# Whitened 2-D convolution: the last three channel groups image by image, x in three tiles, and 1024 consecutive columns at a time in the last pass

## The chip, the cores and the metric

The kernel runs on one core of one Trainium2 chip. The metric is the device time of one execution in microseconds; the time of a kernel is the median of its runs. A core has five engines that matter here: PE (TensorE, matmuls, with its weight loads shown as PEld), DVE (VectorE), ACT (ScalarE), POOL (GpSimd) and SP (SyncE, which here only issues DMAs). 16 DMA engines carry all transfers, whichever engine issued them.

## The reference

Two layers are computed, on `x` of shape (4, 64, 256, 256): 4 images, 64 channels, 256 x 256 pixels.

Layer 0 is a long convolution per channel. Its kernel is an outer product of two filters of length 256 (`hx` and `hy`, each made by a small network of three sine layers and an exponential decay):

```python
k = jnp.einsum('ijk,imk->ijmk', hx, hy)[0]
k = jnp.transpose(k, (2, 0, 1))
k_f = jnp.fft.rfft2(k, s=(fft_size, fft_size)) / fft_size
u_f = jnp.fft.rfft2(x.astype(jnp.float32), s=(fft_size, fft_size))
y = jnp.fft.irfft2(u_f * k_f, s=(fft_size, fft_size))[..., :L, :L]
out = y + x * bias[:, None, None]
```

Since the kernel is separable, this is a product with a lower triangular Toeplitz matrix along one axis of the image and a second one along the other.

Layer 1 whitens the 64 channels over all images and pixels:

```python
x1 = jnp.transpose(x, (1, 0, 2, 3)).reshape(B, -1)
x1_s = x1[:, ::STRIDE ** 2]
mean1 = jnp.mean(x1_s, axis=-1, keepdims=True)
xc = x1 - mean1
cov = x1_s @ x1_s.T / x1_s.shape[1] + EPS * jnp.eye(B, dtype=x.dtype)
deconv = _isqrt_newton_schulz(cov, N_ITER)
out = deconv @ xc
```

The mean and the covariance are taken from every ninth pixel. The inverse square root of the 64 x 64 covariance comes from five Newton-Schulz iterations. No output can be computed until all images have been through layer 0 and the covariance is complete.

## The kernel before

**Filters.** The two small networks run first (lines 149 to 181) and write the filter taps to DRAM (`g_d`), from where they are read back as Toeplitz blocks.

**Main loop (lines 557 to 601).** The channels are split into 8 groups of 8 (`CG`). A *step* is one group of one image, `steps` holds the 32 of them; each has a tile `xt` of 128 partitions x 8 channels x 2 x 256, which is input and then holds the result. A step is worked in four pieces of two channels, c = 0, 2, 4, 6. In this document **pass k** is the turn of the loop with k = 4 * i + c / 2, for step number i; there are 128. One call of `group` does, interleaved on PE, the first Toeplitz factor for pass k's channels and the second factor for those of pass k - 2 (`pending` holds two). The first product reads `toep[g][:, 0]`, the second `toep[g][:, 1]`. Matmuls use 64 partitions of the contraction at a time, a lower and an upper half (`low`), and the two jobs alternate between the halves. The four blocks of 64 are taken in the order 0, 1, 2, 3 on even passes and 3, 2, 1, 0 on odd ones (`orders`). POOL has only empty instructions there, as fences.

Behind the matmuls of a pass (lines 406 to 418): ACT copies the first product out of PSUM (L409), DVE adds `x * bias` to the second product and writes the result over x (L412), `store` issues two stores of the finished channels to the DRAM buffer `y_d` (L425), and `pack` lets DVE run some of the waiting COPY_PREDICATED operations (L319), which pick every ninth pixel into `samp[n]`, nine per group and image, or twice nine of half the width for groups 6 and 7. Then the loop issues a load of x (`load_x`, L101), a part of a Toeplitz block if `blocks` has one for this pass (L193), and an early load of the last pass if `early` has one (L357).

**The order of the steps.** Groups 0 to 5 each go through all four images; groups 6 and 7 are then done image by image: (6, 0), (7, 0), (6, 1), (7, 1) and so on. An image's channels are complete after its (7, n) step.

**SP's queue.** The engines' order is the order in the text (`manual_schedule`). SP issues, in this order for each pass, the two stores, the x load, the block part and the early load; a DMA that has to wait holds up those behind it.

**Buffers of 16 KB per partition.** Four x tiles (`xpool`; step i uses tile i % 4, and the x load in step i is for step i + 2), three Toeplitz tiles (`tpool`), four sample tiles (`spool`, one per image), two in `epool`, one of which is the scratch area of the filter stage. A Toeplitz block of a group is loaded in eight parts: part // 4 is the factor, part // 2 % 2 the half of the partitions, part % 2 the channels (0 to 3 or 4 to 7).

**The covariance.** `covariance(n)` is 116 matmuls on `samp[n]`; it stands in front of pass 4 * i + 1 of the step with g = 7 and image n + 1, for the last image behind the loop. Then comes `whitening` (a chain of small products), which leaves `W` and `shift`.

**The last pass (lines 618 to 647).** The result of layer 0 lies in `y_d` as 32 pieces of 128 partitions x 4096 columns (2 MB). Each piece is loaded into a tile `yt`, multiplied by W in four rounds of 1024 columns (four matmuls, two PSUM banks, one eviction by ACT, L639, and one by DVE, L640, both into the tile itself), and stored to `out` (L645) by SP or POOL. `homes` is the cycle of 13 buffers that the pieces use: letters e, t, s and i for `epool`, `tpool`, `spool` and `xpool`. A home becomes free when the main loop is done with it, and then again when the piece in it has been stored. Nine pieces are loaded during the main loop (`early`), four behind it.

Of the kernel before, what the change touches and what calls it, by code (L numbers as in the profile page):

```python
# [38 lines left out]
F32 = mybir.dt.float32  # L39
I32 = mybir.dt.int32  # L40
AF = mybir.ActivationFunctionType
ALU = mybir.AluOpType
# [3 lines left out]
NB, C, L = 4, 64, 256  # L46
P, H2 = 128, 2
EMB, ORDER = 33, 64
PIX = L * L
CG = 8  # L50
# [4 lines left out]
EPS = 0.01  # L55
N_ITER = 5
GW = P + L
FP = 4096

TURN = 6.283185  # L60
# [4 lines left out]
def conv_whiten_kernel(ctx: ExitStack, tc: tile.TileContext, a: dict, out: bass.AP):  # L65
    nc = tc.nc
    x = a["x"]

    const = ctx.enter_context(tc.tile_pool(name="const", bufs=1))
    xpool = ctx.enter_context(tc.tile_pool(name="xpool", bufs=4))  # L70
    epool = ctx.enter_context(tc.tile_pool(name="epool", bufs=2))
    spool = ctx.enter_context(tc.tile_pool(name="spool", bufs=NB))
    tpool = ctx.enter_context(tc.tile_pool(name="tpool", bufs=3))
    o1pool = ctx.enter_context(tc.tile_pool(name="o1pool", bufs=4))
# [3 lines left out]
    y_d = [dram.tile([H2 * C, PIX // H2], F32, tag=f"y{n}", name=f"y_d{n}") for n in range(NB)]  # L78
    g_d = dram.tile([P, GW], F32, tag="g", name="g_d")
    g0_d = dram.tile([2 * CG, GW], F32, tag="g0", name="g0_d")  # L80

# [6 lines left out]
    cols = const.tile([P, 4], F32, tag="cols", name="cols")  # L88
# [9 lines left out]
    bias = const.tile([P, C], F32, tag="bias", name="bias")  # L98

    def load_x(t, g, n, c):  # L100
        nc.sync.dma_start(  # L101
            out=t[:, c : c + 2],
            in_=x[n, g][:, c : c + 2],
        )


    steps = [(g, n) for g in range(C // CG - 2) for n in range(NB)]
    steps += [(g, n) for n in range(NB) for g in range(C // CG - 2, C // CG)]

    x_tiles = [xpool.tile([P, CG, H2, L], F32, tag="in", name=f"x{u}") for u in range(4)]  # L110
    for c in range(0, CG, 2):
        load_x(x_tiles[0], *steps[0], c)
        if c == 0:
            nc.sync.dma_start(out=decay, in_=a["decay"])
    nc.sync.dma_start(out=mask, in_=a["mask"])
# [5 lines left out]
    for n in range(NB):  # L121
        t = spool.tile([P, FP], F32, tag="samp", name=f"samp{n}")
        samp.append(
# [9 lines left out]
    def load_pick(lo, hi):  # L133
        for s in range(lo, hi):
            nc.scalar.activation(pick[:, s, :], ident, AF.Copy, scale=rows[:, s : s + 1])

    taps = scratch[:, 11:13, :].rearrange("p a w -> p (a w)")[:, 0:GW]
    nc.gpsimd.memset(taps[:, L:GW], 0.0)  # L140

# [13 lines left out]
    for i in range(3):  # L155
        for u in range(2):
# [3 lines left out]
            arg, k, nxt = (scratch[:, 2 + 3 * i + v, half] for v in range(3))  # L160
# [22 lines left out]
    def new_toeplitz(g):  # L183


        return tpool.tile([P, 2, CG, L], F32, tag="toep", name=f"toep_{g}")

    def load_toeplitz(t, g, f, half, lo=0, hi=CG, issue=nc.sync):
        source, row = (g0_d, f * CG + lo) if g == 0 else (g_d, f * C + g * CG + lo)


        skip = 0 if f == half else HP
        issue.dma_start(  # L193
            out=t[half * HP : (half + 1) * HP, f, lo:hi, skip:],
            in_=bass.AP(
                tensor=source.tensor,
                offset=source.offset + row * GW + skip,
                ap=[[1, HP], [GW, hi - lo], [1, L - skip]],
            ),
        )  # L200
# [126 lines left out]
    def covariance(n):  # L327
# [15 lines left out]

    pieces = [(n, q) for n in range(NB) for q in range(PIX // H2 // FP)]


    homes = [
        {"t": (tpool, "toep"), "s": (spool, "samp"), "i": (xpool, "in"), "e": (epool, "extra")}[k]
        for k in "eetssiistitis"
    ]  # L350

    def load_y(i):

        n, q = pieces[i]
        pool, tag = homes[i % len(homes)]
        t = pool.tile([P, FP], F32, tag=tag, name=f"yi_{n}_{q}")
        nc.sync.dma_start(out=t, in_=y_d[n][:, q * FP : (q + 1) * FP])  # L357
        return t

    def load_next():  # L360
        loaded[len(loaded)] = load_y(len(loaded))
# [7 lines left out]


    blocks = {}
    for g in range(1, C // CG):
        first = 16 * g - 14 if g < C // CG - 1 else 16 * g - 22
        for part in range(8):
            k = first + (part * 12 // 8 if g < C // CG - 2 else part)
            blocks[k // 4, k % 4 * 2] = (g, part)

    early = {
        (26, 4): 1, (27, 0): 1, (27, 4): 1, (28, 0): 1, (29, 2): 1, (30, 0): 1, (31, 0): 1, (31, 2): 1, (31, 4): 1
    }  # L380
    orders = [list(range(L // HP)), list(reversed(range(L // HP)))]

# [174 lines left out]
    with tc.manual_schedule(  # L557
        engines={engines.PE, engines.SP, engines.DVE, engines.Activation, engines.Pool}
    ):
        toep = {0: new_toeplitz(0)}  # L560

        for f, lo, hi in ((0, 0, 2), (0, 2, 4), (0, 4, 6), (1, 0, 2), (0, 6, 8), (1, 2, 4), (1, 4, 8)):
            for half in range(2):
                load_toeplitz(toep[0], 0, f, half, lo, hi, nc.scalar if half else nc.sync)
        for c in range(0, CG, 2):
            load_x(x_tiles[1], *steps[1], c)
        for i, (g, n) in enumerate(steps):
            xt = x_tiles[i % 4]
            for c in range(0, CG, 2):
                item = (g, n, c, xt, [])  # L570
                if g == C // CG - 1 and n > 0 and c == 2:
                    covariance(n - 1)
                if len(pending) == 2:
                    group(item, pending.pop(0))
                else:
                    half_group(item, 0)
                pending.append(item)
                if i == 0 and c == 6:

                    fold = const.tile([P, C], F32, tag="fold", name="fold")  # L580
                    nc.vector.tensor_tensor(fold, ident[:, 0:C], ident[:, C:P], ALU.add)

                    nc.scalar.activation(bf[:, 0:1], samp[0][:, 0, 0, C : C + 1], AF.Sqrt)
                if i == 1 and c < CG - 2:
                    load_pick(c // 2 * 3, c // 2 * 3 + 3)

                if i + 2 < len(steps):
                    load_x(x_tiles[(i + 2) % 4], *steps[i + 2], c)
                if (i, c) in blocks:
                    tg, part = blocks[i, c]  # L590
                    if part == 0:
                        toep[tg] = new_toeplitz(tg)
                    lo = part % 2 * CG // 2
                    load_toeplitz(toep[tg], tg, part // 4, part // 2 % 2, lo, lo + CG // 2)
                for _ in range(early.get((i, c), 0)):
                    load_next()
        g, n, c, yt, _ = pending[0]
        for item in pending:
            half_group(item, 1)
            pack(1.0)  # L600
            store(item)

        pack()
        i15 = place(2 * C, rows=C).rearrange("p (u c) -> p u c", u=2)
        for u in range(2):
            nc.gpsimd.tensor_scalar(i15[:, u], ident[0:C, 0:C], 1.5, None, ALU.mult)  # L606
        ones = place(P, rows=C)
        nc.gpsimd.memset(ones, 1.0)
        for lo in range(CG // 2, CG, 2):
            pack_by_pe(g, n, yt, slice(lo, lo + 2))  # L610
        spin(4)
        covariance(NB - 1)
        while len(loaded) < len(homes):
            load_next()
        W, shift = whitening(i15, ones)


    halves = [slice(u * C, (u + 1) * C) for u in range(2)]
    for i, (n, q) in enumerate(pieces):
        yt = loaded.pop(i)  # L620

        v = yt.rearrange("p (v f) -> p v f", v=2)
        o = out[n, q].rearrange("p (v f) -> p v f", v=2)

        part = 512 if i == 0 else 1024 if i == 1 or i > len(pieces) - 3 else 2048
        for w in range(FP // 1024):


            cols = slice(w * 512, (w + 1) * 512)
            po = [  # L630
                psA.tile([P, 512], F32, tag="psA", name=f"po_{n}_{q}_{w}_{u}") for u in range(2)
            ]
            for k in range(2):
                for u in range(2):
                    nc.tensor.matmul(  # L635
                        po[u][halves[k]], lhsT=W[halves[u]], rhs=v[halves[u], k, cols],
                        start=True, stop=True,
                    )
            nc.scalar.activation(v[:, 0, cols], po[0], AF.Identity, bias=shift)  # L639
            nc.vector.tensor_scalar(v[:, 1, cols], po[1], shift, None, ALU.add)  # L640
            end = (w + 1) * 512
            if end % part == 0:

                issue = nc.sync if i == 0 or i + len(homes) >= len(pieces) else nc.gpsimd
                issue.dma_start(out=o[:, :, end - part : end], in_=v[:, :, end - part : end])  # L645
        if i + len(homes) < len(pieces):
            loaded[i + len(homes)] = load_y(i + len(homes))

# [57 lines left out]
```

## Time and profile before

| What | Value |
|---|---|
| Time, median of 3 runs | 903.03 us (901.62 to 903.9) |
| Span of the profiled execution | 902.1 us |
| PE busy | 781.2 us, 87% of the span, 11928 matmuls |
| DVE busy | 581.5 us, 64% |
| ACT busy | 395.5 us, 44% |
| DMA, all queues | 285.61 MB, mean 317 GB/s |
| L220, matmuls of the main loop | 2 x 5040, 284 ns each |
| L357, loads of the last pass | 32 of 2048 KB, 15.6 us from issue to landing |
| L645, stores of the last pass | 17 of 2048 KB by POOL, 11 of 2048 KB by SP, and smaller ones |
| L193, Toeplitz parts | 192 or 256 KB each, 5.7 and 6.3 us from issue to landing |
| L101, loads of x | 128 of 512 KB, 5.3 us |

The span runs from the first to the last instruction. A busy row counts the time in which an engine works; the digits of a row give the busy share of 40 equal slices of the span in tenths. The chain follows the last instruction back, at each step to what released it. In a timeline a row has the start, the length, the engine (with a q where it is its queue that issues), the line, the operation, what it writes and reads, a count where several are merged, and in brackets the idle time before it and what ended it. In a row of windows come the stretch and its length, then the busy time of PE, PEld, DVE, ACT and POOL with the number of instructions, the granted clock of PE, the mean busy share of the DMA engines and what they moved in GB/s.

### The profile page before, as it was taken

What the parts mean: (1) busy time and instruction counts of PE and PEld (TensorE: products, weight loads), DVE (VectorE), ACT (ScalarE), POOL (GpSimd) and SP (SyncE); (2) the same over time, 40 slices, a digit from 0 to 9 for tenths busy, and PEclk for the clock granted to TensorE, in tenths of its full rate; (3) what the DMA queues carried; (4) which work ended last, traced back from release to release, by engine and by line L of the source; (5) the groups of instructions that cost most, each with busy time, mean ns of one, the idle gap of its engine ahead of it and who ended that gap; (6) DMA issues with size and microseconds to landing.
All of it is one profiled execution on the core that took longest, in us unless ns stands there. A gap on an engine that the chain in (4) does not pass through costs nothing.

```text
span 902.1 us, 28046 instructions
## 1 busy us (share of the span) xinstructions
PE 781.2 (87%) x11928; PEld 647.5 (72%) x11928; DVE 581.5 (64%) x801; ACT 395.5 (44%) x676; POOL 14.5 (2%) x40
## 2 busy tenths in 40 slices
PE   8999999999999999999999999999999565666200
PEld 7999999999999999999999999999533111212000
DVE  3487778877888778877888877877688332233200
ACT  2655554545455555545454444442487232233200
POOL 1000000000000000000000000000010000000000
PEclk9999999999999999999999999999999766866755
DMA  7988889798788888888997899979999999999998
GB/s 209 327 262 252 242 261 271 234 273 251 247 263 261 244 264 259 258 250 267 293 275 241 285 351 356 335 237 390 375 401 429 430 432 432 429 434 430 430 430 355
DMA packets 117912, 285.61 MB, mean 317 GB/s; under 512 B 8891, under 2 KB 91116, under 8 KB 110108
## 3 DMA queue, kind: packets, MB, share of 16 engines
q1 hardware_dynamic: 113436, 244.94, 79.0%
q0 software_dynamic: 3056, 37.95, 10.0%
q8 instruction: 95, 1.56, 0.7%
q10 hardware_dynamic: 1296, 0.93, 0.4%
q14 instruction: 29, 0.24, 0.1%
HBM read 149.35 MB, written 134.44 MB: 315 GB/s over the span
## 4 chain that ended last, share of the span: by engine, by line
PE 74%; DMA 11%; another core or an unknown queue 7%; DVE 0%; issue 0%; SPq 0%; ACT 0%; POOLq 0%; DVEq 0%
PE p L220 64%; DMA out_dram<-yi 5%; DMA yi<-y_d 5%; PE po L635 4%; PE pc L333 2%; PE ph L252 1%; PE pk L300 1%; PE spin L442 1%; DMA toep<-g_d 0%; PE busy L152 0%; PE pm L158 0%; SPq L357 0%; DMA scratch<-in_zw_dram 0%; DVE yi L640 0%
## 5 line engine op out<-in xcount | busy, mean ns | idle before, releaser
L220 PE MATMUL p<-toep,x 64*64 64x64 f32 (+3 forms) x5040 | 579.5, 284 | 0.8 <-issue 0.8
L220 PE MATMUL p<-toep,o 64*64 64x64 f32 (+3 forms) x5040 | 579.5, 284 | 0.0
L220 PEld LDWEIGHTS p<-toep,x 64*128 64x128 f32 (+1 forms) x5040 | 535.7, 166 | 24.4 <-issue 1.3
L220 PEld LDWEIGHTS p<-toep,o 64*128 64x128 f32 (+1 forms) x5040 | 536.7, 166 | 10.7 <-issue 0.2
L409 ACT COPY o<-p 64x512 f32<-64x512 f32 x504 | 292.8, 581 | 294.2 <-PE p L220 286.6
L319 DVE COPY_PREDICATED samp<-mask,x 128x464 f32<-128x464 int32 (+3 forms) x351 | 297.2, 847 | 9.8 <-DVE x L412 0.2
L412 DVE SCALAR_TENSOR_TENSOR x<-x,bias,p 128x512 f32<-128x512 f32 x252 | 179.8, 744 | 121.3 <-PE p L220 117.3
L635 PE MATMUL po<-yi,chain 64*64 64x512 f32 x1024 | 143.7, 720 | 60.4 <-DMA yi<-y_d 60.4
L640 DVE TENSOR_SCALAR yi<-po,shift 128x512 f32<-128x512 f32 x128 | 96.1, 751 | 109.0 <-PE po L635 100.7
L635 PEld LDWEIGHTS po<-yi,chain 64*64 64x64 f32 x1024 | 48.0, 162 | 155.2 <-issue 150.5
L639 ACT ACTIVATE yi<-po,shift 128x512 f32<-128x512 f32 x128 | 88.0, 687 | 116.7 <-PE po L635 116.0
L333 PE MATMUL pc<-samp 128*64 128x65 f32 x464 | 14.9, 223 | 0.0
L333 PEld LDWEIGHTS pc<-samp 128*64 128x64 f32 x464 | 14.3, 137 | 0.3
L645 POOL DMA_DIRECT2D out_dram<-yi x19 | 10.5, 554 | 130.5 <-DMA out_dram<-yi 55.1
L606 POOL TENSOR_SCALAR chain<-ident 64x64 f32<-64x64 f32 x2 | 1.0, 519 | 606.6 <-PE ph L252 606.6
L286 DVE COPY o<-ph 64x256 f32<-64x256 f32 x8 | 3.4, 422 | 9.7 <-PE ph L252 9.6
L152 PE MATMUL busy<-idle 128*128 128x128 f32 x64 | 9.4, 307 | 0.0
L152 PEld LDWEIGHTS busy<-idle 128*128 128x128 f32 x64 | 8.9, 222 | 0.2 <-issue 0.2
L300 PE MATMUL pk<-x,pick 128*128 128x56 f32 (+1 forms) x72 | 8.3, 292 | 0.0
L300 PEld LDWEIGHTS pk<-x,pick 128*128 128x128 f32 x72 | 8.1, 192 | 0.1
L442 PE MATMUL spin<-ident 128*128 128x128 f32 x50 | 7.9, 292 | 0.0
L286 ACT COPY o<-ph 64x256 f32<-64x256 f32 x8 | 2.9, 368 | 10.7 <-DMA toep<-g_d 9.2
(93 smaller groups left out, 77.4 us busy)
## 6 DMA issues: line engine op xcount, KB each, us to landing
x<-in_x_dram SPq DMA_DIRECT2D x128, 512.0 KB, 5.3
y_d<-x SPq DMA_DIRECT2D x256, 256.0 KB, 3.5
yi<-y_d SPq DMA_DIRECT2D x32, 2048.0 KB, 15.6
out_dram<-yi POOLq DMA_DIRECT2D x17, 2048.0 KB, 67.7
out_dram<-yi SPq DMA_DIRECT2D x11, 2048.0 KB, 32.9
toep<-g_d SPq DMA_DIRECT2D x28, 256.0 KB, 6.3
toep<-g_d SPq DMA_DIRECT2D x29, 192.0 KB, 5.7
out_dram<-yi SPq DMA_DIRECT2D x4, 1024.0 KB, 32.8
```

The lines of the kernel that those rows point to most:

```text
L152: nc.tensor.matmul(p, lhsT=idle[:, 0:P], rhs=idle[:, P : 2 * P], start=True, stop=True)
L220: mm = nc.tensor.matmul(ps[q : q + w, m, HP * k : L], lhsT=src[parts, k // 2, m * P + q : m * P + q + w], rhs=t[parts, : stop : -1] if k e ...
L300: nc.tensor.matmul(pk[:, b, :, 0:nj], lhsT=pick[:, (s - b) % STEP, :], rhs=yt[:, cs, b, s : s + STEP * (nj - 1) + 1 : STEP], start=(s == 0 ...
L319: nc.vector.copy_predicated(dst, m, src)
L333: nc.tensor.matmul(pc[half], lhsT=samp[n][:, b, j, 0:C], rhs=samp[n][:, b, j, :], start=(b == 0 and j < 2), stop=(b == H2 - 1 and j >= NJ ...
L409: nc.scalar.copy(o1[to], units[u][0][0][fr])
L412: nc.vector.scalar_tensor_tensor(x2[:, c2 + u], x2[:, c2 + u], bias[:, ch : ch + 1], units[u][1][0], ALU.mult, ALU.add,)
L442: nc.tensor.matmul(p, lhsT=ident, rhs=ident, start=True, stop=True)
L635: nc.tensor.matmul(po[u][halves[k]], lhsT=W[halves[u]], rhs=v[halves[u], k, cols], start=True, stop=True,)
L639: nc.scalar.activation(v[:, 0, cols], po[0], AF.Identity, bias=shift)
L640: nc.vector.tensor_scalar(v[:, 1, cols], po[1], shift, None, ALU.add)
L645: issue.dma_start(out=o[:, :, end - part : end], in_=v[:, :, end - part : end])
```

## The change

Five things change together.

- `LATE = 3`: groups 5, 6 and 7 are done image by image, not only 6 and 7. Step 20 is (5, 0), 21 is (6, 0), 22 is (7, 0), 23 is (5, 1). Image 0 is complete after step 22 rather than 25, image 1 after 25 rather than 27, image 2 after 28 rather than 29. The covariance of image n now stands in front of the second pass of the step with g = 6 and image n + 1: passes 97, 109 and 121 instead of 109, 117 and 125.
- Three x tiles instead of four: the load that step i issues is for step i + 1, not i + 2, and step 0 issues none. `epool` has three tiles instead of two.
- The homes of the last pass are taken in another order, with three spare ones first; there are still 13.
- The block loads have a table of their first passes. Groups 1 to 3 are as before; 4 starts at pass 46 instead of 50, 5 at 57 instead of 66, 6 at 69 (spread over 12 passes) instead of 82, 7 at 82 (one per pass) instead of 90. The early loads of the last pass move to passes 94, 96, 98, 100, 111, 122, 123, 125 and 126, from 106, 108, 110, 112, 117, 120, 124, 125 and 126.
- In the last pass a round takes 1024 consecutive columns of the piece, as two runs of 512, where before it took 512 from each half of the piece. A store so covers one run per partition, and the host undoes another layout.

```diff
+LATE = 3
...
-    xpool = ctx.enter_context(tc.tile_pool(name="xpool", bufs=4))
-    epool = ctx.enter_context(tc.tile_pool(name="epool", bufs=2))
+    xpool = ctx.enter_context(tc.tile_pool(name="xpool", bufs=3))
+    epool = ctx.enter_context(tc.tile_pool(name="epool", bufs=3))
...
-    steps = [(g, n) for g in range(C // CG - 2) for n in range(NB)]
-    steps += [(g, n) for n in range(NB) for g in range(C // CG - 2, C // CG)]
-
-    x_tiles = [xpool.tile([P, CG, H2, L], F32, tag="in", name=f"x{u}") for u in range(4)]
+    steps = [(g, n) for g in range(C // CG - LATE) for n in range(NB)]
+    steps += [(g, n) for n in range(NB) for g in range(C // CG - LATE, C // CG)]
+
+    x_tiles = [xpool.tile([P, CG, H2, L], F32, tag="in", name=f"x{u}") for u in range(3)]
+
+    def x_of(i):
+        return x_tiles[(i + 1) % 3]
+
...
-        for k in "eetssiistitis"
+        for k in "eeessstititis"
...
     blocks = {}
-    for g in range(1, C // CG):
-        first = 16 * g - 14 if g < C // CG - 1 else 16 * g - 22
+    for g, (first, groups) in {
+        1: (2, 12), 2: (18, 12), 3: (34, 12), 4: (46, 12), 5: (57, 12), 6: (69, 12), 7: (82, 8)
+    }.items():
         for part in range(8):
-            k = first + (part * 12 // 8 if g < C // CG - 2 else part)
-            blocks[k // 4, k % 4 * 2] = (g, part)
+            k = first + part * groups // 8
+            blocks.setdefault((k // 4, k % 4 * 2), []).append((g, part))
 
     early = {
-        (26, 4): 1, (27, 0): 1, (27, 4): 1, (28, 0): 1, (29, 2): 1, (30, 0): 1, (31, 0): 1, (31, 2): 1, (31, 4): 1
+        (23, 4): 1, (24, 0): 1, (24, 4): 1, (25, 0): 1, (27, 6): 1, (30, 4): 1, (30, 6): 1, (31, 2): 1, (31, 4): 1
     }
...
-            load_x(x_tiles[1], *steps[1], c)
+            load_x(x_of(1), *steps[1], c)
         for i, (g, n) in enumerate(steps):
-            xt = x_tiles[i % 4]
+            xt = x_of(i)
             for c in range(0, CG, 2):
                 item = (g, n, c, xt, [])
-                if g == C // CG - 1 and n > 0 and c == 2:
+                if g == C // CG - 2 and n > 0 and c == 2:
                     covariance(n - 1)
...
-                if i + 2 < len(steps):
-                    load_x(x_tiles[(i + 2) % 4], *steps[i + 2], c)
-                if (i, c) in blocks:
-                    tg, part = blocks[i, c]
+                if 0 < i < len(steps) - 1:
+                    load_x(x_of(i + 1), *steps[i + 1], c)
+                for tg, part in blocks.get((i, c), ()):
...
-        v = yt.rearrange("p (v f) -> p v f", v=2)
-        o = out[n, q].rearrange("p (v f) -> p v f", v=2)
-
-        part = 512 if i == 0 else 1024 if i == 1 or i > len(pieces) - 3 else 2048
+        v = yt.rearrange("p (w v f) -> p w v f", v=2, f=512)
+
+        part = 1024 if i == 0 else 2048 if i == 1 or i > len(pieces) - 3 else 4096
...
-                        po[u][halves[k]], lhsT=W[halves[u]], rhs=v[halves[u], k, cols],
+                        po[u][halves[k]], lhsT=W[halves[u]], rhs=v[halves[u], w, k],
...
-            nc.scalar.activation(v[:, 0, cols], po[0], AF.Identity, bias=shift)
-            nc.vector.tensor_scalar(v[:, 1, cols], po[1], shift, None, ALU.add)
-            end = (w + 1) * 512
+            nc.scalar.activation(v[:, w, 0], po[0], AF.Identity, bias=shift)
+            nc.vector.tensor_scalar(v[:, w, 1], po[1], shift, None, ALU.add)
+            end = (w + 1) * 1024
             if end % part == 0:
...
-                issue.dma_start(out=o[:, :, end - part : end], in_=v[:, :, end - part : end])
+                issue.dma_start(out=out[n, q][:, end - part : end], in_=yt[:, end - part : end])
...
-    y = np.asarray(r.results[0]["out_0_dram"]).reshape(NB, PIX // H2 // FP, H2, C, H2, FP // 2)
-    return np.ascontiguousarray(y.transpose(0, 3, 4, 1, 2, 5)).reshape(NB, C, L, L)
+    y = np.asarray(r.results[0]["out_0_dram"]).reshape(NB, PIX // H2 // FP, H2, C, FP // 1024, H2, 512)
+    return np.ascontiguousarray(y.transpose(0, 3, 5, 1, 4, 2, 6)).reshape(NB, C, L, L)
```

More of the change, by code (lines that the diff above doesn't have):

```diff
@@ L104, in load_x @@
         )
-    steps = [(g, n) for g in range(C // CG - 2) for n in range(NB)]
-    steps += [(g, n) for n in range(NB) for g in range(C // CG - 2, C // CG)]
-    x_tiles = [xpool.tile([P, CG, H2, L], F32, tag="in", name=f"x{u}") for u in range(4)]
+    steps = [(g, n) for g in range(C // CG - LATE) for n in range(NB)]
[3 more added lines that the diff above has]
+        return x_tiles[(i + 1) % 3]
     for c in range(0, CG, 2):
-        load_x(x_tiles[0], *steps[0], c)
+        load_x(x_of(0), *steps[0], c)
         if c == 0:
@@ L620, in conv_whiten_kernel @@
         yt = loaded.pop(i)
-        v = yt.rearrange("p (v f) -> p v f", v=2)
-        o = out[n, q].rearrange("p (v f) -> p v f", v=2)
-        part = 512 if i == 0 else 1024 if i == 1 or i > len(pieces) - 3 else 2048
+        v = yt.rearrange("p (w v f) -> p w v f", v=2, f=512)
+        part = 1024 if i == 0 else 2048 if i == 1 or i > len(pieces) - 3 else 4096
         for w in range(FP // 1024):
-            cols = slice(w * 512, (w + 1) * 512)
             po = [
```

## The prediction

> **What bounds the kernel now.** I read the busy rows by slice first, then the chain that ended last and the waits, then windows on both sides of 645 us, and last the SP queue's timeline around the moment whose lead the change shortens. Passes are numbered k = 4i + c/2 as in the section on the kernel.
>
> The first rows are 40 slices of 22.6 us.
>
> ```profile
> PE   8999999999999999999999999999999565666200
> PEclk9999999999999999999999999999999766866755
> DMA  7988889798788888888997899979999999999998
> ...
> PE 74%; DMA 11%; another core or an unknown queue 7%; DVE 0%; issue 0%; SPq 0%; ACT 0%; POOLq 0%; DVEq 0%
> PE p L220 64%; DMA out_dram<-yi 5%; DMA yi<-y_d 5%; PE po L635 4%; PE pc L333 2%; PE ph L252 1%; PE pk L300 1%; PE spin L442 1%; DMA toep<-g_d 0%; PE busy L152 0%; PE pm L158 0%; SPq L357 0%; DMA scratch<-in_zw_dram 0%; DVE yi L640 0%
> ```
>
> There are two regimes. PE is full until about slice 28 and the chain lies on L220; behind it DMA is at 9 in each slice but the last, and the chain alternates between loads and stores of the last pass. The waits of PE say the same: in the main loop none adds up to a microsecond.
>
> ```profile
> PE po L635 <- DMA yi<-y_d: 60.4, 16, 6.3
> ...
> PE ph L252 <- DMA toep<-g_d: 0.9, 1, 0.9
> PE p L220 <- issue: 0.8, 2, 0.5
> ```
>
> In the windows the last two figures are the DMA share and GB/s.
>
> ```profile
> 590.00:600.00 10.00, 10.00 (x235) 9.41 (x234) 8.88 (x16) 4.65 (x8) 0.00 (x0) 1.00 0.39 128
> 600.00:645.00 45.00, 43.83 (x584) 39.43 (x580) 27.18 (x68) 10.24 (x27) 1.15 (x3) 1.00 1.00 389
> 645.00:650.00 5.00, 5.00 (x52) 1.79 (x48) 4.43 (x7) 4.02 (x7) 0.00 (x0) 1.00 0.70 260
> 650.00:665.00 15.00, 15.00 (x144) 5.36 (x140) 13.07 (x19) 11.92 (x19) 3.05 (x5) 1.00 1.02 372
> 665.00:890.00 225.00, 121.84 (x824) 40.19 (x816) 78.08 (x104) 71.42 (x104) 7.48 (x14) 0.73 1.01 430
> ```
>
> All 13 early pieces have a home before the first store (13 letters in `homes`). Their transfers run at capacity from 600 to 645; then comes a dip to 0.70, because the loads are in and the first store, issued by SP at 645.6, has just begun. From there 32 pieces of 2.1 MB go out and 19 come in: 51 x 2.1 = 107 MB, at 430 GB/s 249 us, which from 646 gives 895 of a span of 902.1. So the end is the start of the last pass plus a fixed amount of transfer, plus whatever of the 13 loads is still owed then. The change keeps 13 homes and every byte. It can gain by an earlier start or by filling the dip, and lose by a later start or by owed loads.
>
> **The change part by part.** *The last Toeplitz block.* Group 7 is now met at step 22, pass 88; its eight loads move from passes 90 to 97 (first use 100) to 82 to 89. They can't move further at one per pass: the buffer was group 4's, read until pass 81. Part 6 (second factor, upper half, first four channels) is issued behind pass 88, and pass 90 multiplies by it: k = 0 comes first on even passes, and its second matmul reads the upper half. One pass lies between. In the trace of before, at the same pass, SP issues the same part of group 6, behind the same two stores and one x load, so it can be read off. The stretch starts with pass 88's stores.
>
> ```profile
> 423.71 0.88 SPq L425 DMA_DIRECT2D y_d<-x  x2
> 424.69 1.43 SPq L101 DMA_DIRECT2D x<-in_x_dram  x1
> 426.17 0.58 SPq L193 DMA_DIRECT2D toep<-g_d  x1
> 427.92 0.88 SPq L425 DMA_DIRECT2D y_d<-x  x2
> ```
>
> The DVE row tells when pass 89 ended; the other is the landing of the 56 block loads from 30 to 470 us.
>
> ```profile
> 426.25 1.64 DVE L412 SCALAR_TENSOR_TENSOR x<-x,bias,p 128x512 f32<-128x512 f32 x2 [2.56 <-PE p L220]
> ```
> ```profile
> DMA to landing us min/median/max: 4.9/6.1/7.5
> ```
>
> The second eviction of pass 89 (0.74 us long, ending at 427.9) starts at 427.1, when PE has finished it, and pass 90 follows at once, at 427.0. The part lands at 426.17 + 6.1 = 432.3, so PE stands still for 5.2 us. Bounds: issued as promptly behind its stores as at pass 92 (443.52 - 442.05 = 1.5 us rather than 2.5), landing in 4.9: 3.1 us; landing in 7.5: 6.7. Behind the waiting matmul stands all of PE's queue; with it evictions, stores and the covariances slip, so the whole amount arrives at the first store. Part 7 is needed two passes behind its issue, 9.2 us and the stall: free.
>
> The Trainium skill's page "DMA: Bandwidth & Descriptors" (section "Anatomy of one DMA") fits a transfer at 2.0 us plus bytes over 436 GB/s, for POOL's queue. For this 256 KB part that would be an estimated 2.6 us, and a stall of 1.8 instead of 5.2; the row of 56 loads, in a queue that is never empty, measures 6.1.
>
> *Loads of the last pass.* Before: passes 106, 108, 110, 112, 117, 120, 124, 125, 126. After: 94, 96, 98, 100, 111, 122, 123, 125, 126. The first four come earlier and gain nothing, since nothing uses them before the start; the same seven have been issued by pass 124. But the sixth and seventh come at 122 and 123 rather than 117 and 120, so they no longer use the idle DMA time between (share 0.39 from 590 to 600). A piece takes 2.1 MB / 430 = 4.9 us. A pass's two stores take 1.6 (128 GB/s at share 0.39 for 0.52 MB), an x load 1.2. From the issue at pass 122 (the store of pass 121 leaves SP at 583.3, one pass of 4.6 and 1.6 for SP's order behind it, and 3.6 for the covariance that now lies ahead: 593.1) to 599.35, where before issues its seventh load: 6.2 us of time for 9.8 + 3.2 + 2.4 = 15.4 of work. Owed: 9.2, against 4.9 in before: 4.3 more at the start of the last pass. It first fills the dip, 0.30 x 5 = 1.5 us. Net +2.8. Bounds: 0, if contention before 600 hid more idle time than I count; 4.3, if the dip is no loss of capacity.
>
> *x in three tiles.* The tile that step i fills was last used by step i - 2 in both kernels, so the wait for evictions, stores and copy_predicated is unchanged. The lead shrinks from eight passes to four. An x load is issued 1.8 us behind its pass; four passes of 4.6 less the pass itself leave 11.8 us. Landing takes 4.9 to 6.5 in the middle of the loop. Around before's own burst of piece loads, from 505 to 560 us, it takes this:
>
> ```profile
> DMA to landing us min/median/max: 4.3/7.9/10.0
> ```
>
> So 1.8 us remain at the worst: 0, with a bound of 2 for one landing missing from the trace. Step 0 no longer loads x: 2.1 MB leave the first 35 us, where PE waits only 0.9 us on a block issued earlier; 0 (bound -0.5).
>
> *The work lists.* The covariances move with their image (passes 97, 109, 121); copy_predicated gets nine wide operations (0.99 us) where two rounds of nine narrow ones (0.62) stood for group 5, on DVE, which has room (8.9 of 10 us). Its last list, which ends the loop, is groups 6 and 7 of the last image in both: 0.
>
> *1024 columns at a time.* Same matmuls (1024 of 589 ns), evictions and bytes; only the runs of the first and last two pieces become twice as long. From 650 to 665 the rate is 372 against 430: 15 x (1 - 372/430) = 2.0 us lost. Taking half back: -1.0, bounds 0 and -2.0. The skill's page (section "Why small descriptors are slow") gives about 3 extra cycles a packet: for 2 KB runs made 4 KB (67 x 2 against 131 cycles) an estimated 2% of one piece, 0.1 us; no row of before separates this cause from others.
>
> Sum: 5.2 + 2.8 - 1.0 = +7.0 on the profiled 902.1: 909.1. The median shown is 0.9 above that execution: 910.0.
>
> **Rivals.** (a) *No stall, loads late:* part 6 lands in time, because SP runs ahead or the queues are shorter in after. For: 1.43 us of SP's delay goes to issuing the x load before it. Against: even the lower bound leaves 3.1. Time: 903.0 + 2.8 - 1.0 = 904.8, no measurable change. (b) *Faster, by a start of the last pass at full rate:* the dip and the 372 GB/s behind it are one thing, an empty queue that is refilled in short runs; with long runs, and transfers still queued, the stretch from 645 to 665 runs at 430. Price -1.5 - 2.0: 903.0 - 3.5 = 899.5. It decides only where stall and owed loads together stay below 0.8 us. For: both rows show the loss. Against: nothing but an early landing of part 6 removes the stall, and after that the tail holds 249 us of transfer whatever comes earlier. (c) *x late, on top of the forecast:* from the point where two pieces lie ahead of an x load in the queue it lands beyond its 11.8 us. That can happen in the burst at passes 94 to 100; two such loads at the bound of 2 us each give 910.0 + 4 = 914. For: 10.0 seen. Against: 10.0 is still inside, and no block loads share the queue then.
>
> **How the numbers follow.** Forecast 0.54, (a) 0.18, (b) 0.14, (c) 0.14. The likeliest's own range is 903.0 + 3.1 + 0 - 2.0 = 904.1 to 903.0 + 6.7 + 4.3 = 914.0. Reaching toward (a) and a little beyond (c), and leaving out (b): 902 to 915. A measurement tells 0.3%, 2.7 us, from no change: below 900.3 is faster (0.14, all of (b)), above 905.7 slower; the forecast's lower edge goes to no change: same 0.21, slower 0.65.
>
> **What would show it.** A wait of PE at L220 for `toep<-g_d` of 3 to 7 us near 427, and no other above 1; the first store of the last pass near 651; no dip at that place, and a seventh piece load issued within one pass of the sixth. I am wrong if PE has no idle time near 427, if idle time sits before several x loads, or if share 1.0 is reached before the sixth load.

## The result, and the profile after

| What | Before | After |
|---|---|---|
| Time, median of 4 runs | 902.98 us (901.62 to 903.9) | 910.81 us (909.44 to 912.64) |
| Ratio, with its 95% interval | | 1.0091 (1.0073 to 1.0109) |
| Span of the profiled execution | 902.1 us | 909.7 us |
| Last pass of the main loop (127) ends | 613.6 us | 620.9 us |
| First store of the last pass issued | 645.6 us | 652.6 us |
| First store to the end of the span | 256.5 us | 257.1 us |
| Last packet of the 13th early load | 646.5 us | 656.7 us |

The change costs 7.8 us. The table says at once where: the first store is 7.0 us later, and what comes behind it takes 0.6 us longer. Ends of passes and packets are read from the trace's instructions and DMA records; some 1.6 us of the comparison are chance, since the profiled execution of before reached pass 89 at 427.1 and those of three variants with the same front (the third, fourth and eighth experiment) at 425.4 to 425.5, as after did. In these three the first store left at 643.6 to 643.8, so against them after's is almost 9 us later.

The slices of after, the same rows as shown of before:

```profile
PE   8999999999999999997999999999999465566300
PEclk9999999999999999999999999999999867767755
DMA  7788788788889888889599869779999999999998
```

PE has one slice at 7, the 19th (409 to 432 us), and DMA falls to 5 in the one behind it: no pass is finished, so nothing is stored and few loads are issued. The waits of PE name the cause, and show a second one:

```profile
PE po L638 <- DMA yi<-y_d: 61.6, 15, 7.5
PE p L225 <- DMA toep<-g_d: 4.8, 1, 4.8
PE pm L163 <- DMA scratch<-in_zw_dram: 2.6, 1, 2.6
PE p L225 <- issue: 2.0, 1, 2.0
```

Line 2 is the forecast stall, once, 4.8 us. Line 4 is a stop of 2.0 us for which the profile has no releaser; in before the same line was 0.8 in two pieces.

First the stall. SP's timeline behind pass 88, and the first product of pass 90 that reads the awaited half:

```profile
422.04 0.87 SPq L431 DMA_DIRECT2D y_d<-x  x2
422.96 0.50 SPq L102 DMA_DIRECT2D x<-in_x_dram  x1
423.50 0.58 SPq L198 DMA_DIRECT2D toep<-g_d  x1
426.50 0.87 SPq L431 DMA_DIRECT2D y_d<-x  x2
```
```profile
430.67 0.76 PE L225 MATMUL p<-toep,o 64*128 64x256 f32 x1 [4.85 <-DMA toep<-g_d]
```

The part is issued 1.5 us behind the stores (the prediction's prompt bound, not the 2.5 that I took) and lands 7.0 us later by the trace (I took 6.1): 430.5, and PE goes on at 430.67. Now that row's second figure, 0.76 us for a matmul of a kind that took 0.38 before. One-microsecond windows of after, with PE's granted clock third from the end:

```profile
427.00:428.00 1.00, 0.00 (x0) 0.00 (x0) 0.94 (x2) 0.03 (x1) 0.00 (x0) 1.00 0.86 238
428.00:429.00 1.00, 0.00 (x0) 0.00 (x0) 0.88 (x2) 0.00 (x0) 0.00 (x0) 0.87 1.05 318
429.00:430.00 1.00, 0.00 (x0) 0.00 (x0) 0.00 (x0) 0.00 (x0) 0.00 (x0) 0.50 1.04 337
...
433.00:434.00 1.00, 1.00 (x8) 0.95 (x6) 0.00 (x0) 0.00 (x0) 0.00 (x0) 0.50 0.10 27
434.00:435.00 1.00, 1.00 (x8) 1.00 (x8) 0.00 (x0) 0.00 (x0) 0.00 (x0) 0.50 0.00 0
435.00:436.00 1.00, 1.00 (x11) 1.00 (x10) 0.00 (x0) 0.00 (x0) 0.00 (x0) 0.72 0.03 8
436.00:437.00 1.00, 1.00 (x19) 1.00 (x16) 0.00 (x0) 0.00 (x0) 0.00 (x0) 1.00 0.00 0
```

The clock falls to half at 428.7, three microseconds into the wait, and stays there until 435.6, five microseconds past its end. The pairs of 256-column matmuls start every 0.43 us (431.22, 431.65, 432.08), where before's first pass had 0.21 (22.35, 22.57, 22.79). PE looks fully busy meanwhile. At half speed that costs an estimated (435.6 - 430.7) / 2 = 2.5 us. Pass 90 lasts 12.6 us in after (425.2 to 437.9) and 4.7 in before: 7.9 for one late transfer, of which the wait and the clock explain all but some 0.6. The Trainium skill's page "TensorE: Matmul & The Clock Gate" (table "Why this matters for your kernels") warns of this, "No PE-idle gaps >~3µs between matmul bursts"; here a gap of 4.85 us had it, and the one of 2.0 shown next had not. The measurements do not bear out 3 us as the bound, though: two experiments below have half clock behind gaps of 1.9 and 2.3 us.

The second stop is in pass 97, right behind the covariance of image 0. Windows of after there:

```profile
469.00:470.00 1.00, 0.47 (x19) 0.33 (x19) 0.23 (x1) 0.00 (x0) 0.00 (x0) 1.00 1.12 405
470.00:471.00 1.00, 0.00 (x0) 0.00 (x0) 0.00 (x0) 0.00 (x0) 0.00 (x0) 1.00 1.01 394
471.00:472.00 1.00, 0.58 (x15) 0.51 (x17) 0.00 (x0) 0.00 (x0) 0.00 (x0) 1.00 1.07 386
```

PE, DVE and ACT all stand, the x of the pass has been there for more than 10 us (its last packet ended at 458.2), and the DMA share is at 1.0 or above: the first piece of the last pass is just through (its packets run from 462.2 to 469.0).

Last, the windows around the start of the last pass, the same stretches as before:

```profile
590.00:600.00 10.00, 10.00 (x176) 9.46 (x174) 6.74 (x8) 4.39 (x8) 0.00 (x0) 1.00 0.39 123
600.00:645.00 45.00, 43.83 (x641) 41.12 (x638) 34.40 (x69) 13.46 (x30) 1.11 (x3) 1.00 1.02 398
645.00:650.00 5.00, 5.00 (x37) 4.06 (x38) 1.82 (x12) 0.78 (x4) 0.00 (x0) 1.00 1.01 433
650.00:665.00 15.00, 15.00 (x140) 5.61 (x144) 11.94 (x17) 11.09 (x17) 1.67 (x3) 1.00 1.02 415
665.00:890.00 225.00, 129.60 (x892) 42.80 (x884) 84.33 (x113) 77.14 (x113) 8.55 (x16) 0.76 1.01 428
```

No dip remains: transfers are still owed when the first store is issued at 652.6, 4.1 us of them (656.7), where before had 0.9.

### The profile page after: what moved, and what is told of

It reads as the page before. It is cut to its first block, busy times and chain, and to the rows that moved or that the text cites. A ratio compares the mean times of both kernels' runs of the same rounds, so it can differ in the third digit from the quotient of the medians.

```text
span 909.7 us, 28015 instructions
## 1 busy us (share of the span) xinstructions
PE 783.9 (86%) x11928; PEld 648.8 (71%) x11928; DVE 580.5 (64%) x801; ACT 395.1 (43%) x676; POOL 14.2 (2%) x40
## 4 chain that ended last, share of the span: by engine, by line
PE 74%; DMA 10%; another core or an unknown queue 9%; DVE 1%; issue 1%; SPq 0%; ACT 0%; POOLq 0%; DVEq 0%
PE p L225 63%; DMA out_dram<-yi 5%; PE po L638 4%; DMA yi<-y_d 3%; PE pc L338 2%; PE ph L257 1%; PE busy L157 1%; PE pk L305 1%; DMA toep<-g_d 1%; PE spin L448 1%; PE pm L163 0%; SPq L362 0%; DMA scratch<-in_zw_dram 0%; DVE yi L643 0%
## 6 DMA issues: line engine op xcount, KB each, us to landing
y_d<-x SPq DMA_DIRECT2D x256, 256.0 KB, 3.5
toep<-g_d SPq DMA_DIRECT2D x28, 256.0 KB, 6.0
```

## The experiments

Each kernel was timed beside before on the same chip. The last column is the difference of the medians of that chip; before was 902.54 us for the first four, 903.11 for the next four, 902.87 for the last four. Kernels that ran on different chips are compared by this column, in which after has +7.8.

| Experiment | Ratio to before (95%) | Median, us | Difference |
|---|---|---|---|
| e1 after, block 7 in six passes | 1.0026 (1.0016 to 1.0036) | 904.67 | +2.1 |
| e2 after, wait filled | 1.0095 (1.0081 to 1.0109) | 911.17 | +8.6 |
| e3 before, long runs | 0.9990 (0.9981 to 0.9999) | 901.64 | -0.9 |
| e4 before, two loads later | 1.0008 (0.9999 to 1.0016) | 903.11 | +0.6 |
| e5 e1, first loads behind the covariance | 0.9985 (0.9976 to 0.9994) | 901.44 | -1.7 |
| e6 before, block 7 late | 1.0079 (1.0065 to 1.0092) | 909.38 | +6.3 |
| e7 e6, wait filled | 1.0100 (1.0087 to 1.0114) | 912.18 | +9.1 |
| e8 before, x in three tiles | 1.0000 (0.9991 to 1.0008) | 903.16 | 0.0 |
| e9 after, first loads behind the covariance | 1.0069 (1.0055 to 1.0083) | 909.24 | +6.4 |
| e10 e9, wait filled | 1.0061 (1.0049 to 1.0074) | 908.24 | +5.4 |
| e11 e1, instructions shifted | 1.0135 (1.0115 to 1.0155) | 915.02 | +12.1 |
| e12 e3, loads behind the covariance | 0.9986 (0.9977 to 0.9994) | 901.58 | -1.3 |

### The late block: e1 and e6

e1 takes the stall out of after with one number:

```diff
-        ... 7: (82, 8)
+        ... 7: (82, 6)
```

> After with one number changed: the eight parts of group 7's Toeplitz block are spread over six passes (82 to 87) instead of eight, so part 6 is issued behind pass 86 and lands, about 9 us after that pass, before pass 90 begins. Theory (the stall at pass 90 and what follows from it on PE is 7.9 us and goes whole into the end): 910.8 - 7.9 = 903, between 902 and 904, no wait of L225 for toep. Rival (the tail would end as late anyway, because loads are owed at the start of the last pass): 907 to 910. A wait that only moves to another part: 910.

904.67 us, +2.1 where after has +7.8: 5.7 gained, not the full 7.9, and above the 902 to 904 expected. The wait for `toep` is gone from the main loop; the other stop is not:

```profile
PE p L225 <- issue: 2.1, 2, 2.0
PE ph L257 <- DMA toep<-g_d: 0.9, 1, 0.9
```

e6 puts the stall into before, where nothing else is changed:

```diff
-        first = 16 * g - 14 if g < C // CG - 1 else 16 * g - 22
+        first = 16 * g - 14 if g < C // CG - 1 else 16 * g - 18
```

> Before with one thing of after alone: group 7's block is loaded as late against its use as there, from pass 94 instead of 90, so that part 6 is issued behind pass 100 for pass 102. Theory (a wait of 4 to 6 us, then PE at half clock for some 5 us, all of it paid at the end): 902.5 + 7 to 8, 909.5 to 910.5. Rival (only the wait counts): 907 to 908. Rival (the tail swallows it, because DMA idle time before the last pass is used in the meantime): 903 to 905.

909.38, +6.3 on its own before. In its profile the wait is 4.0 us:

```profile
PE p L220 <- DMA toep<-g_d: 4.0, 1, 4.0
```
```profile
480.00:485.00 5.00, 1.03 (x10) 0.61 (x8) 3.90 (x7) 2.03 (x4) 0.00 (x0) 1.00 0.94 289
485.00:490.00 5.00, 5.00 (x39) 4.90 (x40) 0.00 (x0) 0.00 (x0) 0.00 (x0) 0.66 0.47 120
```

The clock is at half for 3.4 us this time (485.2 to 488.6), 1.7 us lost, and pass 102 ends at 491.3, where e3, with the same main loop, ends it at 485.0: 6.3. What the pass loses is here what the time loses, 6.3 of which only 4.0 are the wait. The stall is shown from both sides, put in and taken out, and the rival of a tail that swallows it is out. Its size varies from execution to execution, among other things with how long the clock stays down: 6.8 us in after, 3.4 in e6 and in e9 below.

### The fill: e2, e7 and e10 with e9

```diff
+                if 4 * i + c // 2 == 90:
+                    spin(17)
                 if len(pending) == 2:
                     group(item, pending.pop(0))
```

This is e2's edit to after, and e10's to e9; in e7, which starts from e6, the pass is 102. `spin(17)` is 17 products of the identity whose result nobody reads.

> After with 17 products of the identity put on PE in front of pass 90 (0.26 us each in the profile of before, 4.4 us in all), which fill the wait for the block part and change nothing else. Theory (4.85 us of the 7.9 are the wait, and 2.5 are PE at half its granted clock from 428.7 to 435.6, because it stood idle): the clock stays at 1.0 around 430, pass 90 is over 2 to 3 us earlier, time 908 to 909. Rival (the slow stretch has nothing to do with PE's idleness, or the fill only delays PE): 910.8 or more.

> The kernel before this one with 17 products of the identity put on PE in front of pass 102, 4.4 us that fill the wait. Theory (half of the cost beside the wait is the clock): granted clock 1.0 throughout, pass 102 over 2.5 to 3 us earlier, time 906.5 to 907.5. Rival (the clock falls for another reason, or the time is lost elsewhere): as the kernel without the fill, 909.5 to 910.5.

Both times the fill did what it should at its own place and the kernel got no faster: e2 has +8.6 where after has +7.8, and e7 has +9.1 where e6 has +6.3. In e2 the clock stayed at 1.0 there, and pass 90 ended 2.9 us earlier than in after (435.0 against 437.9); in e7 pass 102 ended 1.4 us earlier than in e6. Then the covariance gave it back. In e2 the stop near pass 97 grew to 2.3 us, and e7 got one of 1.9 us at pass 109, where e6 had 0.25; behind each of them the clock was at half for 3.4 us (469.2 to 472.6 and 524.1 to 527.5). A wait row of e2, then one of e7 with its windows:

```profile
PE pc L338 <- issue: 2.7, 2, 2.3
```
```profile
PE p L220 <- issue: 1.9, 1, 1.9
```
```profile
520.00:525.00 5.00, 3.08 (x77) 2.81 (x74) 1.78 (x4) 0.00 (x0) 0.00 (x0) 0.91 1.03 385
525.00:530.00 5.00, 5.00 (x44) 4.74 (x44) 1.07 (x2) 1.13 (x2) 0.00 (x0) 0.75 1.05 444
```

The 17 products wait for no load; what they shift is the place of all later instructions of PE, and by one the turn of the eight PSUM tiles (`psA`), of which they take one. So the pair e9 and e10 was run with the first piece loads moved out of that neighbourhood; the edit to after is

```diff
-        (23, 4): 1, (24, 0): 1, (24, 4): 1, (25, 0): 1,
+        (24, 4): 1, (25, 0): 1, (25, 4): 1, (26, 0): 1,
```

> After with only the first four loads of the last pass moved behind the covariance (98, 100, 102, 104); group 7's block stays late. A control for the next one. Theory: the stall at pass 90 stays whole (4.9 us of wait, pass 90 12.5 us long), the stop at pass 97 is gone: 901.4 + 7.9 = 909, between 908 and 910.

> The kernel before this one with 17 products in front of pass 90, which fill the wait; there is no load of the last pass near to collide with. Theory (half clock costs 2.5 us of the stall): clock 1.0 throughout, pass 90 ends near 435, 2 to 3 us below the control, 906 to 907. Rival (the fill brings nothing to the end): as the control, 909.

909.24 and 908.24. The fill now gains 1.0 us, with intervals that overlap, not the 2 to 3 expected. In the profiled executions the control waited 3.9 us and had half clock for only 3.4 us (from 430.0, ended 433.4), and pass 90 ended 0.6 us later than with the fill (436.0 against 435.4). But e10 has stops of 0.5 and 0.6 us at the first two covariances, where e9 has none, and its first store is the later one (649.6 against 648.5). That the clock is lost to the wait is shown (it never fell in a filled wait, and it fell in each unfilled one); what that alone costs the kernel's time is not, since no fill made a kernel faster clear of noise.

### The stop behind the covariance: e5 and e11

e5 is e1 with the diff of e9:

> After with group 7's block spread over passes 82 to 87, as in the first experiment, and the first four loads of the last pass moved from passes 94, 96, 98, 100 to 98, 100, 102, 104, behind the covariance of image 0 at pass 97. Open is a stop of PE for 2.0 us at pass 97 in after, in the first experiment, and of 2.3 us in the second, which the profile gives no releaser for. Theory (PE runs through its instructions twice as fast in the covariance, and the fetch of the next ones waits behind the first 2 MB piece: in after the fetch starts at 469.1, when the piece's packets end, 11 us behind the one before): the stop is gone or at most 0.5 us, the first store near 643.8, time 902 to 903. Rival (it belongs to the covariance, or to a bank, and not to the loads): 2 us of idle time remain at pass 97, 904.5.

901.44 us, less than the 902 to 903 expected: the stop is gone, and the kernel is 1.7 us below before (ratio 0.9976 to 0.9994). PE is busy throughout the stretch that holds pass 97:

```profile
465.00:480.00 15.00, 15.00 (x282) 14.02 (x280) 13.60 (x17) 7.54 (x14) 0.00 (x0) 1.00 0.75 248
```

So the long stop needs more than the covariance. e9 says the same of after: with the loads moved, its waits have no row for such a stop either. e11 leaves e1's loads where they are and shifts the instruction stream:

```diff
     busy(22)
+    few = psA.tile([P, P], F32, tag="psA", name="few")
+    for _ in range(32):
+        nc.tensor.matmul(few[:, 0:1], lhsT=idle[:, 0:P], rhs=idle[:, P : P + 1], start=True, stop=True)
```

> The first experiment's kernel (block early, first loads at 94 to 100, a stop of 2.0 us at pass 97) with 32 products of one column more on PE ahead of the main loop. Each is four instructions, 128 in all, half of a 16 KB block of them at 64 bytes each; they shift where in the loop PE's next instructions are fetched, and nothing else in it. Theory (the stop is a fetch held behind the first piece load): the fetch that stood at 461.9 comes before or after that load, the stop at pass 97 is below 0.5 us; the time is 904.7 - 2 plus up to 4 us for the added products, 904 to 907. Rival (the stop comes from the loads in another way, as through x or a bank): 2 us of idle time remain.

The stop is gone here too. The products of the main loop stand on line 228 of this kernel, and its waits of PE have no row for them:

```profile
PE po L641 <- DMA yi<-y_d: 61.9, 16, 6.3
PE pm L163 <- DMA scratch<-in_zw_dram: 2.5, 1, 2.5
PE pq L466 <- DVE chain L512: 0.5, 1, 0.5
```

Its time was misjudged: the 32 short products took 11.6 us (14.7 to 26.3), not 4, at half clock from 17.0 to 30.6, and pass 89 ends some 12 us late; the 915.02 say nothing on the stop. Nor does e11 alone exclude a bank, since `few` takes one of the eight PSUM tiles and shifts their turn by one.

What does point to the fetch are the DMA records of the instruction queue (q8, packets of 16 KB). In the main loops of the 14 traces PE has 15 stops of 0.19 to 2.3 us for which the profile has no releaser, and each of them ends 1.2 to 1.6 us behind the end of such a packet: in after 469.96 and 471.42, in e1 462.85 and 464.10, in e2 466.57 and 467.92, in e7 522.26 and 523.49. The four waits for `toep` end 5 us and more behind one. So PE stood for its instructions. In the four kernels with a long stop that packet is late: it starts 11.0 us behind the one before it in after (458.1 to 469.1), 11.7 in e1 (450.2 to 461.9), 11.3 in e2, 11.0 in e7, each time within 0.6 us of the end of the first piece's packets, and moving the piece load alone removed the stop twice (e1 to e5, after to e9). A gap of that length is no stop by itself; e5 has one of 11.4 (530.3 to 541.7) and loses nothing. Open is how the load holds the packet up: in before and in e11 a fetch starts in the midst of the first piece (512.9 and 468.4) and PE hardly notices, and e10 stops for 0.5 us in a covariance before any piece is issued (466.6 and 479.3). The skill's page "Runtime: NRT & Kernel Launch" (section "Instruction fetch mechanics") has the instructions streamed in blocks of 16 KiB, 256 instructions each, the cost "mostly hidden"; the packets agree in size, and at these places 2 us were not hidden.

### The last pass: e3, e4 and e12

e3 is before with the new rounds of the last pass and the host's layout, e4 is before with two early loads moved:

```diff
-        ... (28, 0): 1, (29, 2): 1, (30, 0): 1, (31, 0): 1,
+        ... (28, 0): 1, (30, 4): 1, (30, 6): 1, (31, 0): 1,
```

> Before with only the last pass changed: 1024 consecutive columns a round, as in after. Theory: the first two pieces go out in runs twice as long, and the stretch behind the first store, 372 GB/s in before, comes to 400 or more; 1 to 2 us gained, 901 to 902. Rival (the rate there is set by the mixture of loads and stores, not by the length of the runs): 903, within 0.5 us of before.

> Before with only two early loads of the last pass moved: the fifth and sixth from passes 117 and 120 to 122 and 123. Nothing changes on PE. Theory (DMA time left idle between 560 and 600 us is lost, and what is owed at the first store is paid at the end, less the dip at 645 us which it fills): the loads end about 4 us later, the dip at 645 to 650 is gone, time +2 to +3, 905 to 906. Rival (that idle time is of no use, as all 13 loads are in before the first store anyway): 903.

e3 gains 0.9 us, at the edge of its interval. Its 15 us behind 650 run at 394 GB/s instead of 372. Before's first store came 1.8 us later, but e4, with the short runs and its first store at the same time as e3's, has 376, so the runs were part of that slowness (e3, then e4):

```profile
650.00:665.00 15.00, 15.00 (x144) 5.36 (x140) 13.07 (x19) 11.92 (x19) 2.56 (x5) 1.00 1.02 394
```
```profile
650.00:665.00 15.00, 15.00 (x145) 5.36 (x140) 13.17 (x18) 11.99 (x18) 2.84 (x5) 1.00 1.01 376
```

e4 loses 0.6 us, not 2 to 3, and its interval includes no loss; its rival is nearer. Its 13 loads end at 645.2, 1.5 us behind the first store (643.7) and not 4, so it is a weak test of what owed loads cost. A window of e4 shows why they end so early:

```profile
600.00:645.00 45.00, 43.81 (x548) 38.65 (x550) 27.94 (x68) 11.49 (x29) 1.10 (x3) 1.00 1.00 409
```

The share from 600 to 645 is 1.00 as in before, but the rate is 409 GB/s where it was 389. A share of 1.00 was not full capacity: with more to load, the same stretch moved 45 x 20 = 0.9 MB more, 2.1 us' worth at 430 GB/s. What sets the rate at that share isn't shown.

e12 is e3 with `(26, 4), (27, 0), (27, 4), (28, 0), (29, 2)` replaced by `(27, 4), (28, 0), (28, 4), (29, 0), (29, 4)`:

> Before with the long runs of the last pass and the first five early loads moved from passes 106, 108, 110, 112, 117 to 110, 112, 114, 116, 118, behind the covariance at 109. An attempt at a version that beats both kernels. Theory: the stop of 0.5 us behind that covariance goes, nothing else is late: 901 to 901.6, at most 0.5 below the long runs alone (901.64). Rival (loads crowd behind pass 118 and more is owed at the first store): 902 to 903.

901.58, 1.3 below the before of its chip. The stop behind the covariance at pass 109 is gone; one of 0.35 us stands behind the next covariance (559.0). The medians of e3, e5 and e12 lie within 0.2 us of each other, those against their own before within 0.8, and their intervals overlap. e5 and e12 both beat before by about 0.15%, and after by some 9 us; between the two nothing is told apart.

### x in three tiles: e8

Before with three x tiles, x loaded one step ahead, three `epool` tiles, and the homes `eeetssistitis`:

```diff
-                if i + 2 < len(steps):
-                    load_x(x_tiles[(i + 2) % 4], *steps[i + 2], c)
+                if 0 < i < len(steps) - 1:
+                    load_x(x_of(i + 1), *steps[i + 1], c)
```

> Before with x in three tiles and three spare buffers, the x load one step ahead instead of two, order of steps, block loads and passes of the early loads as in before; the homes begin with three spare ones. Theory (11.8 us of lead are enough; the smallest margin between an x load's last packet and its pass was 1.7 us in after): no wait of the products for x above 1 us, 902.5 to 903.5. Rival (loads of x land late in the burst of piece loads at passes 106 to 112): waits of 2 us or more there, 905 or more.

903.16, ratio 1.0000. One stop behind the covariance of 0.8 us, no wait for x. In after itself the smallest margin between an x load's last packet and its pass was 1.7 us (pass 127), then 1.8 (pass 105); in before, from pass 8 on, it was 20.

## Why the prediction came out as it did

The forecast was 910.0 and the time is 910.81; its main step is right in place, cause and wait; what else it got wrong erred in opposite directions.

- *Part 6 is late, PE waits 5.2 us, all of it arrives at the end.* Right in place, cause and size: 4.85 us, inside 3.1 to 6.7, and both e1 and e6 show it paid at the end. Both halves of the sum were off by a microsecond and cancelled, which is luck: issue 1.5 us behind the stores instead of 2.5, landing 7.0 instead of 6.1. The fit of the Trainium skill's page "DMA: Bandwidth & Descriptors" (section "Anatomy of one DMA"), which is for POOL's queue, gives this part an estimated 2.6 us and a stall of 1.8; it did not hold for the part as SP issued it here.
- *"Behind the waiting matmul stands all of PE's queue ... so the whole amount arrives."* What was missing is what the wait does to PE itself: the clock. The step priced the stall by its wait alone. Pass 90 lost 7.9 us in after, pass 102 lost 6.3 in e6, for waits of 4.85 and 4.0; by the differences of the table the late block costs 7.8 - 2.1 = 5.7 (after against e1) to 6.4 + 1.7 = 8.1 (e9 against e5).
- *"The first four come earlier and gain nothing."* They gained nothing and cost something: with them ahead of the covariance PE stopped 2.0 us at pass 97. Moving them is worth 7.8 - 6.4 = 1.4 with the block late (after against e9) and 2.1 + 1.7 = 3.8 with it early (e1 against e5). "No other above 1" failed here.
- *Loads owed, +2.8 net.* The mechanism was right (owed 4.1 us in after against 0.9, the dip filled), the term was too large. Of the kernels with long runs, those that owe 3.8 to 4.1 us at the first store (after, e1, e5) need 257.0 to 257.1 from there to the end, and those that owe 0.6 and 1.4 (e3, e12) need 256.2 and 256.0: some 1 us, by one execution each. The step took the share of 1.00 from 600 to 645 us for capacity, though its own row said 389 GB/s beside the 430 of later.
- *Long runs, -1.0.* e3: -0.9, with an interval that reaches almost to 0.
- *x in three tiles, 0.* e8: 0.0, and no trace with three tiles has a wait for x, so rival (c) is out. The smallest margins in after are near the 1.8 worked out, though not in the burst at passes 94 to 100 that it was worked out for.

Late block and first loads together cost 7.8 + 1.7 = 9.5 us, the distance from after to e5, where the forecast had 5.2; the clock and the stop at pass 97 are the 4.3 that it left out. Everything else of the change is e5 itself: -1.7, where the forecast had 2.8 - 1.0 = 1.8, or 3.5 too much. About 2 of these are the owed loads. Some of the rest is a first store 1.4 us ahead of e3's and e4's (642.3 against 643.8 and 643.7), which have a stop of 0.5 and 0.25 us behind their first covariance; what else is in it isn't traced. So 7.0 + 4.3 - 3.5 = 7.8: the forecast is right by its main term, and its accuracy to 1 us is luck.

## What to carry to other kernels

A block that is moved with its use has to be checked at every part, not only at its first: count the passes between the issue of each part and the matmul that reads it. If PE waits there, read the granted clock behind the wait too; here it cost 1.7 to 2.5 us on PE behind waits of 3.9 to 4.85. A DMA share of 1.0 did not mean full capacity here; read the GB/s beside it. A fill or a big load can move a stop instead of removing it, so look at the whole list of waits after each edit, not at the place that was mended.

## What the runs showed of the hardware that I had not expected

- Behind idle times of 3.9, 4.0 and 4.85 us PE ran at half clock until 3.7 to 4.9 us after it had resumed. Two idle times of 1.95 us had no such stretch (after, e1), but one of 1.92 in e7 and one of 2.3 in e2 had: the length alone did not decide. Each time the clock was down for 3.4 us, in after for 6.8.
- 32 products of a single column took 11.6 us, 64 matmuls of 181 ns, though PE's 128-column products before them took 115 ns each (44 in 5.1 us); during them the granted clock fell to 0.50 while PE counted as busy.
- PE stopped for up to 2.3 us for instructions, when the first 2 MB load of a stretch met the covariance, whose 116 matmuls take 3.7 us; each such stop ended 1.2 to 1.6 us behind a 16 KB packet of the instruction queue. A shift by 128 instructions of a stream of thousands removed it.
